# Softplus sums, projected rows and convolution weights in the Mamba stage of a hybrid network

## The chip, the cores and the metric

One core of a Trainium2 chip runs the whole network in one program. The metric is device time in microseconds from start to end of the program; a profiled execution also gives a trace of every instruction. The engines are TensorE (PE, matrix products into PSUM banks; PEld is its weight load), VectorE (DVE), ScalarE (ACT), GpSimd (POOL) and SyncE (SP, which here only issues DMAs). ACT and POOL also have DMA queues.

## The reference

The network has four layers on an image batch of 2 x 256 x 32 x 32. Layer 0 adds two Mamba blocks to a group norm; layer 1 is a 7 x 7 dilated kernel attention; layers 2 and 3 are attention and mixtures of experts. Only layer 0, and the preparation of layer 1's convolution weights that is done beside it, concern the change. Cut to what matters:

```
xr = u @ in_w + in_b                      # u: (b, 1024, 256)
xs, res = split(xr, 2)                    # 512 channels each
xs = silu(depthwise_conv4(xs) + conv_b)
dt, Bm, Cm = split(xs @ xproj_w, [16, 32])
delta = softplus(dt @ dt_w + dt_b)
dA  = exp(delta[..., None] * A)           # A: (512, 16)
dBu = delta[..., None] * Bm * xs[..., None]
h_t = dA_t * h_(t-1) + dBu_t              # scan over the 1024 tokens
y   = sum_n h_t * C_t + xs * Dp
out = (y * silu(res)) @ out_w + out_b
xt  = xt + layernorm(out)                 # twice: m1, then m2 (channels flipped)
```

Layer 1 convolves x with w1 (128 x 256 x 7 x 7), then with w2 (49 x 128); the kernel multiplies the two weights into one set of 49 taps first.

## The kernel before

**Tiling.** The 2048 tokens are four chunks j of 512 (TC). The 512 inner channels are four blocks dc of 128 partitions (NDC = 4). Two blocks of four chunks make eight *units*. Each unit runs `scan`: for each of 16 states n and each dc, ACT makes the decay `da` = exp(delta * A) into PSUM (L468), POOL makes the input `h` = du * b for two dc at once (L461), and VectorE scans h in place (L472). `rest(n)` then transposes h by PE into PSUM banks `ht` (L440, three banks), and VectorE (for two of the n ACT, L447) multiplies by C and adds to `ya` (L449). Six `h` tiles, three `da` banks and four `b` tiles are in turn; `b` comes by SP (L457) from DRAM, where the front has put it.

**Slots.** Each scan is one slot, 64 per unit. In the 63 slots between, `paced` pulls steps of generators: the *front* of the next unit (projection in, convolution, softplus), the *back* of the unit before (gate, skip, projection out, layer norm, residual), the weights of the next block, and `aside`, which is `Taps.make`. Each entry of `steps` is (generator, how many steps, first slot, end slot). The numbers in `layer0` set which work stands near which scan. They give the order in which the program is written; a planner of the framework then orders each engine's instructions by its own estimates of cost, with the written order as the priority, and gives out the buffers. On the chip each engine runs its list in that order.

**The front** (`front`, 22 head steps and 16 softplus steps) computes softplus from x = dt @ dt_w + b as max(x, 0) + ln(1 + e) with e = exp(-|x|). To keep the digits of small e, it adds e - ((e + 1) - 1). `e` lies in the buffer tag `pre`, `ln` in the tag `gate`, and `w` in `du` (one, one and two buffers). The four operations of each dc are at L405 (w = e - w), L407 (ln + w), L409 (delta + ln) and L411 (delta * xs); they run on POOL, except in the very first front (`alone`), where nothing else runs yet and VectorE does them. The rounding step is two ACT operations (L403, L404), or one on VectorE if alone.

**The back** (`back`) takes 9 steps for gate and y in slots 0 to 35 and 7 more in slots 40 to 61: four products into two PSUM banks of the pool `ps_mm` (tag `mm`, two banks for all matmul results), then `net.norm_rows` over the four row tiles straight from those banks (L160, L161 statistics, L150 square root, L151 and L166 factors, L168 result into `o`), then two steps of transposing (L179), scaling (L540) and adding to `xt` on POOL (L543, and L548 for the second block).

**Convolution weights** (`Taps.make`): 28 parts of four (or two) 128 x 128 pieces. Each part is loaded by SP (L686, two loads ahead), transposed by PE (L700), copied by ACT (L702) in one step; in the next step it is multiplied with w2 (L706), copied (L711) and written to DRAM by SP (L714). The last unit's `load` reads these rows back (L740) into the buffers of pre, xs, delta and du, for `convolve` (L762), which runs beside the last scan and, with `both`, beside the last back: there one step of the back is pulled after every three convolution steps.

Of the kernel before, what the change touches and what calls it, by code (L numbers as in the profile page):

```python
# [233 lines left out]
class Mamba:  # L234
# [58 lines left out]
    def front(self, j, alone=False):  # L293
# [104 lines left out]
        for dc in range(NDC):  # L398
            w = du[:, dc, :]
            if alone:  # L400
                nc.vector.tensor_scalar(w, e[:, dc, :], 1.0, -1.0, ALU.add, ALU.add)
            else:
                nc.scalar.activation(w, e[:, dc, :], AF.Identity, bias=net.one)  # L403
                nc.scalar.activation(w, w, AF.Identity, bias=net.minus_one)  # L404
            eng.tensor_sub(w, e[:, dc, :], w)  # L405
            yield
            eng.tensor_add(ln[:, dc, :], ln[:, dc, :], w)  # L407
            yield
            eng.tensor_add(delta[:, dc, :], delta[:, dc, :], ln[:, dc, :])  # L409
            yield  # L410
            eng.tensor_mul(w, delta[:, dc, :], xs[:, dc, :])  # L411
            yield
# [72 lines left out]
    def back(self, j):  # L485
# [33 lines left out]
        found = []  # L519
        for i in range(TPC):  # L520
# [11 lines left out]
            found.append(a)  # L532
            yield
        tiles = [o[:, i, :] for i in range(TPC)]
        net.norm_rows(tiles, found, nc.scalar)
        yield
        for cc in range(NCC):
# [37 lines left out]
def layer0(net, x, x_dram, m1, m2, load_image, taps, conv_dram, lg):  # L575
# [5 lines left out]
    with (  # L581
# [32 lines left out]
        for u, (m, j) in enumerate(units):  # L614
# [48 lines left out]
class Taps:  # L663
# [11 lines left out]
    def make(self, psum, dram):  # L675
# [17 lines left out]
        for i, (u, k) in enumerate(parts):  # L693
# [3 lines left out]
            n = min(4, 14 - k)  # L697
# [3 lines left out]
            wt = pool.tile([P, TC], F32, tag="w1t", name=f"w1ts_{u}_{k}", bufs=1)  # L701
# [8 lines left out]
            out = pool.tile([P, 4, NTAP], F32, tag="taps", name=f"taps_sb_{u}_{k}", bufs=3)  # L710
# [3 lines left out]
            nc.sync.dma_start(self.made[u][:, k : k + n, :], out[:, :n, :])  # L714
# [1028 lines left out]
```

## Time and profile before

| | |
|---|---|
| median of 3 runs | 2186.85 us (2185.29 to 2189.43) |
| the profiled execution | 2188.29 us, its span 2186.6 us |
| first scan, last scan | 53.3 us, 1030 us |
| starts of the eight units | 53.3, 165.3, 292.3, 418.75, 543.2, 664.4, 789.1, 913.8 us |
| last back and end of the first convolution | 1034 to 1110 us |
| VectorE in 52 to 1036 us | 925.2 us busy |
| ACT in 52 to 1036 us | 681.5 us busy |
| POOL in 52 to 1036 us | 768.9 us busy |
| softplus on POOL, L405, L407, L409, L411 | 28 each; 1184, 1273, 1271, 1273 ns |
| h on POOL, L461 | 254; 2364 ns |
| decay on ACT, L468 | 512; 690 ns |

How to read it: a group's line in the profile names the source line, the engine, the operation, the tile written and the tiles read, the shapes and the count; then busy time and the mean of one in ns; then how long the engine stood idle just before such instructions, and which instruction's end released it. The table by stretches lists busy time (and instructions) of PE, PEld, DVE, ACT and POOL, the granted clock of PE as a share of full speed, the DMA share and GB/s. In the timeline a line is a start, a duration, the engine, the line and the tiles.

### The profile page before, as it was taken

How to read it: one execution, taken by the hardware profiler on the slowest of the kernel's cores; microseconds unless marked ns; L12 is line 12 of the kernel's file. 1: busy time of each engine (PE TensorE's matmuls, PEld its weight loads, DVE VectorE, ACT ScalarE, POOL GpSimd, SP SyncE). 2: the span in 40 equal slices, each digit the busy share in tenths (PEclk: the TensorE clock that was granted, in tenths of full speed). 3: DMA queues.
4: the chain of work that ended last, by engine and by line, in shares of the span. 5: the costliest groups of instructions: out<-in, count | busy, mean ns of one | idle time of the engine just before them, and what ended most of it. 6: DMA issues, size and time to landing. Idle time of an engine off the chain costs nothing.

```text
span 2186.6 us, 27311 instructions
## 1 busy us (share of the span) xinstructions
PE 1894.0 (87%) x9652; PEld 1335.5 (61%) x9652; DVE 1400.3 (64%) x2210; ACT 959.2 (44%) x1610; POOL 1028.9 (47%) x726
## 2 busy tenths in 40 slices
PE   6888898898978888788999989949999599859996
PEld 2464555556555655454646556539999467649995
DVE  6999998999999999899005475752222544432223
ACT  4676677767777767645013454411111132301111
POOL 3796787959698686965025420012332000023331
PEclk9869889898989889899999999969999799979997
DMA  2121121111212111310030100028998200059997
GB/s 106 45 68 39 37 69 35 58 35 45 62 47 60 38 49 35 85 42 17 0 64 1 48 15 10 20 82 306 326 329 323 82 10 10 20 206 327 329 323 292
DMA packets 90499, 223.87 MB, mean 102 GB/s; under 512 B 35467, under 2 KB 51728, under 8 KB 79732
## 3 DMA queue, kind: packets, MB, share of 16 engines
q1 hardware_dynamic: 77636, 198.29, 27.1%
q0 software_dynamic: 7728, 19.15, 2.9%
q10 hardware_dynamic: 4992, 4.59, 0.7%
q8 instruction: 81, 1.33, 0.3%
q14 instruction: 62, 0.51, 0.1%
HBM read 204.60 MB, written 19.37 MB: 102 GB/s over the span
## 4 chain that ended last, share of the span: by engine, by line
PE 32%; DVE 22%; issue 19%; POOL 11%; ACT 10%; DMA 5%; POOLq 0%; SPq 0%; DVEq 0%; ACTq 0%
DVE m_h L472 11%; DVE m_ya L449 6%; PE acc L762 3%; POOL x L1520 3%; POOL l_yd L1570 3%; PE m_ht L440 3%; PE early_acc L762 3%; PE av L1276 3%; ACT m_da L468 2%; PE sc L1250 2%; DMA l_yd<-y,target 2%; POOL m_h L461 2%; PE h L1099 2%; PE m_xd_ps L351 1%; PE w L1108 1%
## 5 line engine op out<-in xcount | busy, mean ns | idle before, releaser
L461 POOL TENSOR_TENSOR m_h<-m_du,m_b 128x1024 f32<-128x1024 f32 x254 | 594.5, 2364 | 196.0 <-PE m_ht L440 95.8
L440 PE MATMUL m_ht<-ident,m_h 128*128 128x128 f32 x2048 | 361.2, 305 | 119.4 <-DVE m_ya L449 83.9
L440 PEld LDWEIGHTS m_ht<-ident,m_h 128*128 128x128 f32 x2048 | 259.5, 154 | 317.8 <-DVE m_ya L449 112.7
L468 ACT ACTIVATE m_da<-m_delta,m_aneg 128x512 f32<-128x512 f32 x512 | 349.5, 690 | 220.8 <-DVE m_h L472 220.1
L1520 POOL DMA_INDIRECT x<-l_zd,source x82 | 84.8, 1034 | 573.1 <-DVE source L1465 217.1
L449 DVE SCALAR_TENSOR_TENSOR m_ya<-m_ht,m_ct,m_ya 128x512 f32<-128x512 f32 x448 | 320.2, 733 | 18.4 <-PE m_ht L440 17.5
L472 DVE TENSOR_TENSOR_SCAN m_h<-m_da,m_state,m_h 128x512 f32<-128x512 f32 x256 | 318.7, 1271 | 14.7 <-POOL m_h L461 8.7
L472 DVE TENSOR_TENSOR_SCAN m_h<-m_da,m_h 128x512 f32<-128x512 f32 x256 | 303.3, 1210 | 23.6 <-ACT m_da L468 13.1
L1550 PEld LDWEIGHTS h<-xts,we 128*128 128x128 f32 x2528 | 298.4, 194 | 7.1 <-issue 3.4
L1550 PE MATMUL h<-xts,we 128*128 128x128 f32 x2528 | 299.4, 277 | 2.2 <-issue 1.7
L1557 DVE TENSOR_TENSOR hid<-hid,h 128x512 f32<-128x512 f32 x79 | 54.3, 688 | 258.9 <-PE h L1550 258.9
L1556 ACT ACTIVATE hid<-h 128x512 f32<-128x512 f32 x79 | 47.2, 598 | 384.6 <-issue 324.0
L1564 PE MATMUL o<-we,hid 128*128 128x256 f32 x632 | 150.4, 380 | 2.2 <-DVE y L1569 1.6
L1570 POOL DMA_INDIRECT l_yd<-y,target x79 | 79.3, 1003 | 142.6 <-DVE y L1569 136.3
L1564 PEld LDWEIGHTS o<-we,hid 128*128 128x128 f32 x632 | 113.7, 190 | 15.7 <-DVE y L1569 2.8
L336 PE MATMUL m_conv<-m_pre,m_taps 128*128 128x512 f32 x240 | 114.6, 596 | 6.7 <-ACT m_gate L498 5.6
L762 PE MATMUL early_acc<-x,early 128*98 128x448 f32 (+21 forms) x308 | 97.0, 447 | 0.0
L762 PE MATMUL acc<-x,pair 128*98 128x416 f32 (+21 forms) x308 | 93.6, 452 | 0.0
L1569 DVE COPY y<-o 128x256 f32<-128x256 f32 x79 | 33.6, 425 | 69.6 <-PE o L1564 69.6
L309 PE MATMUL m_in<-x,m_in_sb 128*128 128x512 f32 x128 | 68.8, 663 | 9.8 <-ACT m_pre L313 6.9
L762 PEld LDWEIGHTS acc<-x,pair 128*98 128x98 f32 x308 | 47.7, 167 | 39.9 <-issue 34.5
L528 PE MATMUL m_out<-m_out_sb,m_xs 128*128 128x256 f32 x256 | 68.7, 397 | 0.0
(318 smaller groups left out, 2843.3 us busy)
## 6 DMA issues: line engine op xcount, KB each, us to landing
we<-in_l_experts_dram SPq DMA_DIRECT2D x82, 1536.0 KB
m_b<-m_bd SPq DMA_DIRECT2D x128, 256.0 KB
w<-in_l_w_dram SPq DMA_DIRECT2D x21, 256.0 KB
l_zd<-l_z SPq DMA_DIRECT2D x7, 512.0 KB
l_yl<-l_yd SPq DMA_DIRECT2D x10, 256.0 KB
l_yl<-l_yd ACTq DMA_DIRECT2D x10, 256.0 KB
early<-taps SPq DMA_DIRECT2D x7, 343.0 KB
pair<-taps SPq DMA_DIRECT2D x7, 343.0 KB
```

The source lines that it names most:

```text
L309: nc.tensor.matmul(ps, lhsT=self.in_sb[:, kc, mc * P : (mc + 1) * P], rhs=self.xt[:, kc, tok], start=(kc == 0), stop=(kc == NCC - 1),)
L336: nc.tensor.matmul(ps, lhsT=self.taps[:, dc * 4 + k, :], rhs=pre[:, dc, k : k + TC], start=(k == 0), stop=(k == 3),)
L440: nc.tensor.transpose(ps[:, dc * P : (dc + 1) * P], hs[dc // G][:, dc % G, i * P : (i + 1) * P], net.ident,)
L449: nc.vector.scalar_tensor_tensor(ya[:, i, :], ps, c, ya[:, i, :], ALU.mult, ALU.add)
L461: (nc.vector if start and n == 0 else nc.gpsimd).tensor_mul(h, du[:, g * G : (g + 1) * G, :], b.unsqueeze(1).to_broadcast(half))
L468: nc.scalar.activation(da, delta[:, dc, :], AF.Exp, scale=self.aneg[:, i : i + 1])
L472: nc.vector.tensor_tensor_scan(h, da, h, 0.0 if first else state[:, n, dc : dc + 1], ALU.mult, ALU.add)
L762: nc.tensor.matmul(a[:, lo - 16 * k : hi - 16 * k, co : co + n], lhsT=lhsT, rhs=self.x[:, kc, b, lo - r0 : hi - r0, ci : ci + n], start=(u ...
L1520: nc.gpsimd.indirect_dma_start(out=x, out_offset=None, in_=zd[:, :], in_offset=bass.IndirectOffsetOnAxis(ap=source[:, g : g + 1], axis=0), ...
L1550: nc.tensor.matmul(ps[:, at], lhsT=w12[:, s, kc, at], rhs=xt[:, kc * P : (kc + 1) * P], start=(kc == 0), stop=(kc == NCC - 1),)
L1564: nc.tensor.matmul(ps[:, :C], lhsT=ht[:, mc * P : (mc + 1) * P], rhs=w[:, 8 + mc, :], start=(mc == 0), stop=(mc == NHC - 1),)
L1570: nc.gpsimd.indirect_dma_start(out=yd[g], out_offset=bass.IndirectOffsetOnAxis(ap=target[:, g : g + 1], axis=0), in_=y, in_offset=None, bo ...
```

## The change

- Softplus: e - ((e + 1) - 1) is now got as e plus (1 - (e + 1)) on ACT. The three additions per dc become one PSUM sum on PE: identity matmuls of delta, e, ln and w into a bank of `ps_mm`. ACT copies the bank to `delta`; POOL keeps the product with xs. The 12 steps stand in slots 38 to 54.
- In the first front, VectorE keeps the subtraction, PE sums delta, ln and w (banks of `ps_ht` for odd dc), and VectorE multiplies straight from PSUM.
- The back copies each pair of projected rows out of PSUM to `o` by ACT as soon as it is complete. Statistics are taken from `o`, one row tile per step; the factors and the in-place results are steps of their own. It has ten steps in slots 38 to 62 instead of seven in 40 to 61.
- `Taps.make` uses 35 parts of three (or two) pieces; the rows are written by the ACT queue; ten (twelve in the first unit) steps stand in slots 24 to 63 instead of nine (twelve) in 40 to 63.

```diff
             if alone:
                 nc.vector.tensor_scalar(w, e[:, dc, :], 1.0, -1.0, ALU.add, ALU.add)
+                nc.vector.tensor_sub(w, e[:, dc, :], w)
             else:
                 nc.scalar.activation(w, e[:, dc, :], AF.Identity, bias=net.one)
-                nc.scalar.activation(w, w, AF.Identity, bias=net.minus_one)
-            eng.tensor_sub(w, e[:, dc, :], w)
-            yield
-            eng.tensor_add(ln[:, dc, :], ln[:, dc, :], w)
-            yield
-            eng.tensor_add(delta[:, dc, :], delta[:, dc, :], ln[:, dc, :])
-            yield
-            eng.tensor_mul(w, delta[:, dc, :], xs[:, dc, :])
+                nc.scalar.activation(w, w, AF.Identity, scale=-1.0, bias=net.one)
+            yield
+
+            pool, tag = (self.ps_ht, "ht") if alone and dc % 2 else (self.ps_mm, "mm")
+            ps = pool.tile([P, TC], F32, tag=tag, name=f"{m}_sp_{j}_{dc}")
+            parts = (delta, ln, du) if alone else (delta, e, ln, du)
+            for k, a in enumerate(parts):
+                nc.tensor.matmul(
+                    ps, lhsT=net.ident, rhs=a[:, dc, :], start=(k == 0), stop=(k == len(parts) - 1)
+                )
+            nc.scalar.copy(delta[:, dc, :], ps)
+            yield
+            eng.tensor_mul(w, ps if alone else delta[:, dc, :], xs[:, dc, :])
             yield
...
         o = self.one.tile([P, TPC, C], F32, tag="o", name=f"{m}_o_{j}")
-        found = []
+        tiles = [o[:, i, :] for i in range(TPC)]
+        mv = net.small.tile([P, TPC, 2], F32, tag="ln_mv", name="ln_mv")
+
+        def stats(i):
+            st = net.small.tile([P, 6], F32, tag="ln_st", name="ln_st")
+            nc.vector.bn_stats(out=st, in_=tiles[i])
+            nc.vector.bn_aggr(out=mv[:, i, :], in_=st)
+
...
-            found.append(a)
-            yield
-        tiles = [o[:, i, :] for i in range(TPC)]
-        net.norm_rows(tiles, found, nc.scalar)
+
+            if i % 2:
+                nc.scalar.copy(
+                    o[:, i - 1 : i + 1, :], ps.rearrange("p (i c) -> p i c", c=C)
+                )
+            if i > 1:
+                stats(i - 2)
+            yield
+        stats(2)
         yield
+        stats(3)
+        rs = net.small.tile([P, TPC], F32, tag="ln_rs", name="ln_rs")
+        net.rstd(rs, mv[:, :, 1])
+        off = net.small.tile([P, TPC], F32, tag="ln_off", name="ln_off")
+        nc.vector.scalar_tensor_tensor(off, mv[:, :, 0], -1.0, rs, ALU.mult, ALU.mult)
+        yield
+        for i, a in enumerate(tiles):
+            nc.scalar.activation(
+                a, a, AF.Identity, scale=rs[:, i : i + 1], bias=off[:, i : i + 1]
+            )
+            if i % 2:
+                yield
...
-            steps += [(f, 16, 38, 62) for f in fronts] + [(b, 7, 40, 61) for b in done]
+            steps += [(f, 12, 38, 54) for f in fronts] + [(b, 10, 38, 62) for b in done]
             steps += [(rest, 1, 62, 63)]
             if u + 1 < len(units):
-                n = 9 if u else 12
-                steps += [(islice(aside, n), n, 40, 63)]
+                n = 10 if u else 12
+                steps += [(islice(aside, n), n, 24, 63)]
...
-        parts = [(u, k) for u in range(7) for k in range(0, 14, 4)]
+        parts = [(u, k) for u in range(7) for k in range(0, 14, 3)]
...
-            n = min(4, 14 - k)
-            w = pool.tile([P, 4, P], F32, tag="w1", name=f"w1_{u}_{k}", bufs=3)
+            n = min(3, 14 - k)
+            w = pool.tile([P, 3, P], F32, tag="w1", name=f"w1_{u}_{k}", bufs=3)
             nc.sync.dma_start(
-                w[:, :n, :], self.w1[:, u, k // NCC : (k + n) // NCC].rearrange("p v c o -> p (v c) o")
+                w[:, :n, :], self.w1[:, u].rearrange("p v c o -> p (v c) o")[:, k : k + n]
             )
...
-            nc.sync.dma_start(self.made[u][:, k : k + n, :], out[:, :n, :])
+            nc.scalar.dma_start(self.made[u][:, k : k + n, :], out[:, :n, :])
```

More of the change, by code (lines that the diff above doesn't have):

```diff
@@ L696, in make @@
             w = loaded[i]
-            n = min(4, 14 - k)
+            n = min(3, 14 - k)
             ps = psum.tile([P, TC], F32, tag="mm", name=f"w1t_{u}_{k}")
@@ L700, in make @@
                 nc.tensor.transpose(ps[:, a * P : (a + 1) * P], w[:, a, :], net.ident)
-            wt = pool.tile([P, TC], F32, tag="w1t", name=f"w1ts_{u}_{k}", bufs=1)
+            wt = pool.tile([P, 3 * P], F32, tag="w1t", name=f"w1ts_{u}_{k}", bufs=1)
             nc.scalar.copy(wt[:, : n * P], ps[:, : n * P])
@@ L709, in make @@
                 )
-            out = pool.tile([P, 4, NTAP], F32, tag="taps", name=f"taps_sb_{u}_{k}", bufs=3)
+            out = pool.tile([P, 3, NTAP], F32, tag="taps", name=f"taps_sb_{u}_{k}", bufs=3)
             nc.scalar.copy(
```

## The prediction

> **What bounds the kernel now.** I read the busy times first, then the stretch that the change touches, then who waits in it, and last the timeline of a few unit ends.
>
> ```profile
> PE 1894.0 (87%) x9652; PEld 1335.5 (61%) x9652; DVE 1400.3 (64%) x2210; ACT 959.2 (44%) x1610; POOL 1028.9 (47%) x726
> ...
> 52.00:1036.00 984.00, 838.63 (x3893) 531.55 (x3892) 925.15 (x1063) 681.46 (x1102) 768.93 (x417) 0.89 0.17 48
> ```
>
> The second line is the table by stretches (columns PE, PEld, DVE, ACT, POOL). Over the whole span PE looks like the bound; inside layer 0's scans (52 to 1036 us) VectorE is, with 925 of 984 us. The change touches only this layer.
>
> ```profile
> L449 DVE SCALAR_TENSOR_TENSOR m_ya<-m_ht,m_ct,m_ya 128x512 f32<-128x512 f32 x448 | 320.2, 733 | 18.4 <-PE m_ht L440 17.5
> L472 DVE TENSOR_TENSOR_SCAN m_h<-m_da,m_state,m_h 128x512 f32<-128x512 f32 x256 | 318.7, 1271 | 14.7 <-POOL m_h L461 8.7 <-ACT m_da L468 5.9
> L472 DVE TENSOR_TENSOR_SCAN m_h<-m_da,m_h 128x512 f32<-128x512 f32 x256 | 303.3, 1210 | 23.6 <-ACT m_da L468 13.1 <-POOL m_h L461 10.5
> ```
>
> VectorE's work is scans and sums, which the change leaves alone. What it can win is the idle before them: 18.4 + 14.7 + 23.6 and 1.9 before L516, 58.6 us together. The waits split it:
>
> ```profile
> DVE m_h L472 <- POOL m_h L461: 19.2, 13, 4.9
> DVE m_h L472 <- ACT m_da L468: 19.0, 23, 2.5
> DVE m_ya L449 <- PE m_ht L440: 17.5, 26, 2.2
> ```
>
> Then where. I cut each of the eight units (first scans at 53.3, 165.3, 292.3, 418.75, 543.2, 664.4, 789.1, 913.8; end 1034) into its 64 slots and took VectorE's busy time per stretch. For the fifth unit, slots 38-46, 46-54, 54-62 and 62-64:
>
> ```profile
> 615.20:630.30 15.10, 13.40 (x80) 10.36 (x79) 13.88 (x20) 15.04 (x22) 15.02 (x9) 1.00 0.14 40
> 630.30:645.50 15.20, 9.32 (x44) 5.94 (x42) 14.78 (x20) 11.13 (x22) 14.96 (x10) 0.78 0.24 77
> 645.50:660.60 15.10, 12.72 (x73) 11.07 (x72) 12.96 (x17) 10.12 (x22) 14.83 (x11) 0.66 0.10 32
> 660.60:664.40 3.80, 3.07 (x15) 2.02 (x16) 3.13 (x5) 3.03 (x9) 3.72 (x4) 1.00 0.32 109
> ```
>
> POOL has no pause, VectorE loses 2.14 + 0.67 = 2.81 us in the last ten slots, and PE pauses in the second stretch. The last ten slots of the first seven units lose 2.02, 2.14, 2.78, 2.22, 2.81, 2.09 and 4.50 us, and the first twelve slots of the last two units 2.67 and 1.88: 23.1 us lost at **hand-overs**. Slots 38-54, the **middle**, lose 0.8, 3.3, 1.7, 1.9, 1.6, 1.6 and 1.1: 12.0 us. One hand-over closely:
>
> ```profile
> 908.70 1.28 POOL L409 TENSOR_TENSOR m_delta<-m_delta,m_ln 128x512 f32<-128x512 f32 x1
> 910.06 1.27 POOL L411 TENSOR_TENSOR m_du<-m_delta,m_xs 128x512 f32<-128x512 f32 x1
> 911.28 4.66 POOL L461 TENSOR_TENSOR m_h<-m_du,m_b 128x1024 f32<-128x1024 f32 x2
> ...
> 910.01 0.69 ACT L498 ACTIVATE m_gate<-m_g,cols_sb 128x512 f32<-128x512 f32 x1 [6.57 <-POOL m_delta L409]
> ...
> 911.32 1.22 DVE L472 TENSOR_TENSOR_SCAN m_h<-m_da,m_h 128x512 f32<-128x512 f32 x1 [2.50 <-ACT m_da L468]
> ```
>
> ACT stood 6.57 us behind POOL's last softplus sum (the gate needs ln's buffer), the decay in its queue behind it came late, and VectorE stood 2.50 us. POOL's softplus chain is what ends last there.
>
> **The change, part by part.** Costs come from these rows:
>
> ```profile
> L405 POOL TENSOR_TENSOR m_du<-m_e,m_du 128x512 f32<-128x512 f32 x28 | 33.2, 1184 | 0.0
> L407 POOL TENSOR_TENSOR m_ln<-m_ln,m_du 128x512 f32<-128x512 f32 x28 | 35.6, 1273 | 1.1
> L409 POOL TENSOR_TENSOR m_delta<-m_delta,m_ln 128x512 f32<-128x512 f32 x28 | 35.6, 1271 | 1.5
> L702 ACT COPY w1ts<-w1t 128x512 f32<-128x512 f32 (+1 forms) x28 | 14.8, 529 | 5.5 <-PE w1t L700 5.1 <-ACT m_state L432 0.2
> ...
> 22.49 7.03 PE L336 MATMUL m_conv<-m_pre,m_taps 128*128 128x512 f32 x16
> ```
>
> (1) POOL loses 12 of its 16 softplus operations per front: 33.2 + 35.6 + 35.6 = 104.4 us, 14.9 us in each of seven units, and the last product is planned eight slots (15 us) earlier. In the last 24 slots (46 us) it then has 12 products of 2.36, 4 of 1.27 and 2 adds of 1.27: 36 us, so it gets ahead. Of the 23.1 us, the waits put down to POOL (19.2 less 6.1 behind the tap diagonals at 344 and 361 us, which stay) are 13.1, and some 8 are decays that came late. Bounds: 8 (a third) to 23.1. I take **-16**, most of what these two explain, because PE and ACT get fuller and some of it returns with another releaser. What is late next there: PE's backlog from (2).
>
> (2) PE gains, per unit, 4 sums of 4 matmuls 128x512. The 16 instructions above took 7.03 us, 0.44 each, and a float matmul is two of them (64 products on L309, 128 instructions): 32 x 0.43 = 13.8 us, 96 us in all. They queue before later transposes (L440), for which L449 waits. PE in slots 38-46 then has 32 transposes (3.9 us, 0.49 per four), 40 out-projection instructions of 0.217 (8.7), two sums (6.9) and some taps (1.0): 20.5 us in 15.2, 5.3 us behind, and catches up until about slot 56, where it now pauses. Cover: three m_ht banks and six m_h tiles, which let VectorE scan on while sums wait. Without cover it is 5.3 less the 1.6 us that PE stands in this stretch, 3.7 per unit, +26. With full cover 0. The nearest row is the stretch of slots 26-38, where PE is 98% busy (22.8 of 23.3 us) and VectorE loses about 2.1 us in twelve slots; the middle loses 1.7 today. ACT belongs here too: per unit 4 copies of the sums and 2 of the out rows at 0.57 and 5 DMA issues at 0.31 (the ACT queue's issue of m_bd), 5 us, in a stretch where it is already 15.04 of 15.10 busy; its decays are queued behind these. I take +1.2 us per unit for both, **+8.4**.
>
> [...] The clock shows 0.66 and 0.78 in the stretches above, and 0.50 from 520 to 535 us, where PE runs mostly L440. [...]
>
> (3) Convolution weights: 35 parts of three instead of 28 of four, from slot 24 on. Copies stay equal (a 384-wide copy for a 512-wide one). Some 3.6 of ten steps, 2 us of PE, move per unit to slots 24-38, where PE is 98% busy; they leave the end, where they crowd. Bounds 0 to 7 x 2 = 14; I take **+2**, since VectorE loses only 2.1 of 23.3 us there. The last nine steps now run in the seventh unit instead of none; their rows are read first in the eighth, behind loads of early tiles that wait for that unit's last product anyway (issued at 918 us). Moving the 35 writes from SP's queue to ACT's: 0 for SP, because POOL never waits for m_b in layer 0; the ACT issues are counted.
>
> [...]
>
> (4) Out rows copied from PSUM: the statistics cost 418 ns from PSUM and 416 from SBUF (L160 on m_out and on t), so no price on VectorE; two banks, held in the second unit from 241 and 254 to 279 us, come free after two steps each, so taps need not crowd into the end (278 to 292 us now). This gain is in (1).
>
> (5) First front: eight VectorE adds of 0.68 go (5.4 us); four sums of three matmuls come, 24 x 0.43 = 10.3 us on PE, which stands from 43 to 50 us. Two of the sums need the m_mm banks, which hold the next front's rows until ACT empties them at 49.3 us behind VectorE's last L405; that one now comes some 4 us earlier. The first scan moves from 53.3 to about 50. Bounds -5.4 to +3 (sums late at half clock); I take **-3**.
>
> (6) End of the layer: the last back half has 19 steps instead of 16, pulled once per three of 56 convolution steps, 18 pulls; the last transposes come behind the convolution (PE never idle 1052 to 1110 us). r, two adds of 1.27 on POOL end near 1114 instead of 1106.3; the next convolution starts at 1116.6 behind its weights' load. Only the xk transposes that fill 1111 to 1116 move back: **+1.5**, bounds 0 to 4.
>
> **The sum**: -16 + 8.4 + 2 - 3 + 1.5 = -7.1 us. The profiled execution took 2188.29 (span 2186.6 and 1.7 around it), 1.4 above the median; its span becomes 2179.5. From the median 2186.85 that is **2180**.
>
> **Rivals.**
> - *PE becomes the bound of the middle.* Place: slots 38-50 of seven units. For it: the 5.3 us of backlog, and ACT at 15.04 of 15.10. Against: slots 26-38 with PE as full lose only 2.1. Price +26 in place of +8.4: 10.5 us slower than before, 2197. It decides from 2.2 us per unit ((16 + 3 - 3.5) / 7).
> - *An even trade.* The planner that orders the instructions lets the sums slip past slot 54, and only 8 us of the hand-overs return: -8 + 8.4 + 2 - 3 + 1.5 = +0.9, 2188. For it: today's last product is planned for slot 61 and ran at slots 61 to 62 (287.0, 660.8 and 910.1 us); against: POOL's 14.9 us are gone wherever the sums land.
> - *Everything is covered*: -23.1 - 3 + 1.5 = -24.6, 2162. Against: PE at 98% has nowhere cost nothing.
>
> **Chances.** Forecast 0.42 (its own range 2168 to 2182), everything covered 0.10, even trade 0.20, PE bound 0.28. A measurement of this kernel tells about 0.2% (4.4 us) from no change: faster 0.52, same 0.20, slower 0.28. The range 2161 to 2198 leaves out about one in ten on the slow side and a little on the fast one.
>
> **What would show it.** Right: POOL with pauses in slots 54-64 and no VectorE wait for L461 there; first scan near 50 us; the clock near 1.00 in slots 46-54; VectorE's idle in layer 0 near 49 us. Wrong: L449 behind L440 well above 17.5 us, or L472 behind L468 above 19.0 in slots 42-50. The prediction fails if the middle loses over 2.2 us more per unit, or if hand-overs keep over half of their 23 us.

## The result, and the profile after

The changed kernel takes **2219.86 us** (median of 4 runs, 2214.84 to 2220.98), the kernel before 2186.07 (4 runs beside it): ratio **1.0151, interval 1.0136 to 1.0166**. It is slower by 1.5%, where the forecast was 2180. The profiled execution took 2214.84 us, the lowest of the four, with a span of 2212.9; it shows 26.3 us of loss against the span of 2186.6 before. The accounts by slots below are of these 26.3 us; the other 7.5 of the 33.8 between the medians stand in no profile. Lines have moved: L440 is now L446, L449 L455, L461 L467, L468 L474, L472 L478, L512 L518, L516 L522. New are L412 (the sums), L415 (their copy), L417 (GpSimd's product) and L530 and L559 (the rows' statistics and factors).

First the page's busy times, then the stretch that holds the scans of layer 0 in the table by stretches:

```profile
PE 1947.8 (88%) x9900; PEld 1349.7 (61%) x9900; DVE 1400.9 (63%) x2202; ACT 987.1 (45%) x1672; POOL 925.1 (42%) x642
```

```profile
50.00:1056.00 1006.00, 884.80 (x4116) 542.35 (x4115) 927.49 (x1061) 706.63 (x1160) 665.93 (x332) 0.96 0.17 47
```

GpSimd is relieved as planned (768.9 to 665.9 us), TensorE gained 46 us, the clock rose from 0.89 to 0.96. VectorE does the same work (925 and 927 us), but its stretch is 22 us longer (1006 against 984). So the loss is idle time of VectorE. The groups and the waits:

```profile
L455 DVE SCALAR_TENSOR_TENSOR m_ya<-m_ht,m_ct,m_ya 128x512 f32<-128x512 f32 x448 | 318.6, 731 | 31.5 <-PE m_ht L446 30.7
L478 DVE TENSOR_TENSOR_SCAN m_h<-m_da,m_state,m_h 128x512 f32<-128x512 f32 x256 | 317.0, 1266 | 16.5 <-POOL m_h L467 9.3
L478 DVE TENSOR_TENSOR_SCAN m_h<-m_da,m_h 128x512 f32<-128x512 f32 x256 | 301.8, 1207 | 27.6 <-POOL m_h L467 14.7
```

```profile
DVE m_ya L455 <- PE m_ht L446: 30.7, 37, 2.9
DVE m_h L478 <- POOL m_h L467: 24.0, 15, 3.6
DVE m_h L478 <- ACT m_da L474: 19.5, 22, 1.8
```

Behind TensorE's transposes VectorE now waits 30.7 us (17.5 before), behind GpSimd's products 24.0 (19.2). Where in a unit, is seen by cutting the eight units into their slots again, as 64 equal parts of each unit's time; VectorE's idle time, summed over the units, in us (each entry is the length of the stretches less VectorE's busy time in them):

| slots | 0-12 | 12-26 | 26-38 | 38-46 | 46-54 | 54-64 | sum |
|---|---|---|---|---|---|---|---|
| before | 5.1 | 9.7 | 12.9 | 7.3 | 4.7 | 19.0 | 58.6 |
| after | 2.0 | 7.3 | 25.9 | 25.1 | 16.0 | 2.3 | 78.5 |

The hand-over is as good as free of idle time now; slots 26 to 54 lose 42 us more. The fifth unit, stretches for slots 26-38, 38-46, 46-54, 54-62 and 62-64 (columns: length, PE, PEld, DVE, ACT, POOL, clock, DMA share, GB/s):

```profile
604.30:628.40 24.10, 20.19 (x104) 12.96 (x103) 19.50 (x24) 12.08 (x25) 14.90 (x10) 0.90 0.17 41
628.40:644.50 16.10, 16.10 (x60) 11.52 (x60) 10.12 (x12) 13.59 (x19) 7.38 (x4) 0.72 0.12 37
644.50:660.50 16.00, 16.00 (x73) 10.45 (x73) 13.81 (x21) 13.49 (x27) 10.59 (x5) 1.00 0.14 41
660.50:676.60 16.10, 14.25 (x89) 10.40 (x88) 15.67 (x21) 13.74 (x28) 14.75 (x9) 1.00 0.41 105
676.60:680.60 4.00, 3.14 (x13) 1.36 (x12) 4.00 (x5) 2.48 (x6) 4.00 (x3) 1.00 0.16 53
```

TensorE is busy for all of 16.10 and all of 16.00 us, while VectorE stands 6.0 and 2.2. In the same stretches before, TensorE worked 13.40 and 9.32. VectorE is busy throughout the last ten slots but for 0.4 us, where it lost 2.81.

Only the seventh unit is like this one: in both, slots 38-46 run at a clock of 0.72 and 0.73, and VectorE loses 8.2 and 8.1 us in slots 38 to 54. The other five units lose 3.8 to 6.7 there; their clock in slots 38-46 is 0.88 to 1.00, and TensorE is not busy all the time in them. The fourth unit, slots 38-46 and 46-54:

```profile
499.80:515.90 16.10, 14.51 (x76) 10.09 (x76) 13.79 (x17) 15.95 (x22) 10.68 (x6) 1.00 0.16 50
515.90:532.00 16.10, 15.46 (x74) 10.29 (x72) 14.20 (x21) 12.35 (x21) 10.32 (x6) 1.00 0.16 51
```

Here ScalarE is the fullest engine in the first stretch (15.95 of 16.10 us). By what VectorE waited for, slots 38 to 54 of the first seven units have 15.7 us behind GpSimd's products (none before), 12.3 behind TensorE's transposes (5.8 before) and 12.8 behind ScalarE's decays (6.8 before). The hand-over into the last unit, in the timeline:

```profile
931.41 0.67 ACT L504 ACTIVATE m_gate<-m_g,cols_sb 128x512 f32<-128x512 f32 x1
...
934.57 2.54 POOL L573 TENSOR_TENSOR x<-x,m_r 128x512 f32<-128x512 f32 x2
...
937.29 2.44 DVE L478 TENSOR_TENSOR_SCAN m_h<-m_da,m_state,m_h 128x512 f32<-128x512 f32 x2
```

The gate on ScalarE no longer stands 6.57 us behind softplus on GpSimd, and the unit's first scan has no idle time before it.

**Where TensorE gets behind.** TensorE's timeline in the same unit, before slot 38:

```profile
617.87 1.05 PE L518 MATMUL m_y<-ident,m_ya 128*128 128x128 f32 x8
618.76 1.06 PE L518 MATMUL m_y<-ident,m_yb 128*128 128x128 f32 x8
619.74 1.12 PE L380 MATMUL m_dt<-m_xd,m_dt_sb 16*128 16x512 f32 x2
620.79 0.77 PE L446 MATMUL m_ht<-ident,m_h 128*128 128x128 f32 x5
623.92 0.90 PE L730 MATMUL w1t<-ident,w 128*128 128x128 f32 x3 [2.37 <-DVE m_xs L522]
624.62 1.91 PE L446 MATMUL m_ht<-ident,m_h 128*128 128x128 f32 x8
...
633.32 3.78 PE L541 MATMUL m_out<-m_out_sb,m_xs 128*128 128x256 f32 x8
```

The weights' transposes (L730), now among the skip products, need one of the two `mm` banks. The bank is held by y until VectorE has multiplied it by the gate (L522), and that stands behind three scans in VectorE's own order. TensorE stands 2.37 us, with transposes of h ready behind L730 in its list. In the whole trace these waits are

```profile
PE w1t L730 <- DVE m_xs L522: 13.2, 8, 4.3
```

After this one the clock is down, seen in the table by stretches:

```profile
622.00:624.00 2.00, 0.07 (x1) 0.08 (x2) 2.00 (x4) 1.32 (x3) 0.03 (x1) 0.92 0.10 26
624.00:627.00 3.00, 3.00 (x12) 2.63 (x13) 1.92 (x3) 1.71 (x4) 1.82 (x1) 0.50 0.25 68
...
633.00:636.00 3.00, 3.00 (x7) 2.19 (x7) 2.28 (x3) 2.97 (x4) 3.00 (x2) 0.50 0.00 1
636.00:638.00 2.00, 2.00 (x12) 1.67 (x11) 0.25 (x1) 1.99 (x3) 0.62 (x1) 0.67 0.10 37
638.00:641.00 3.00, 3.00 (x11) 1.50 (x10) 3.00 (x4) 1.58 (x3) 0.00 (x0) 1.00 0.24 63
```

For 13 us TensorE is wholly busy at half speed; eight products of the out projection take 3.78 us, where they take 1.99 at a clock of 1.00 (sums_rows, 649.50). The sums then follow upon this backlog. The seventh unit repeats it. In the third, a wait of 4.3 us goes with a clock of 0.79 in slots 26 to 38; after the other waits, 0.64 to 1.31 us each, the clock stays at 1.00 for the next 4 us.

### The profile page after: what moved, and what is told of

Same layout as the page of the kernel before. It is cut to its first block, busy times and chain, and to the rows that moved or that the text cites. A ratio compares the mean times of both kernels' runs of the same rounds, so it can differ in the third digit from the quotient of the medians.

```text
span 2212.9 us, 27828 instructions
## 1 busy us (share of the span) xinstructions
PE 1947.8 (88%) x9900; PEld 1349.7 (61%) x9900; DVE 1400.9 (63%) x2202; ACT 987.1 (45%) x1672; POOL 925.1 (42%) x642
## 4 chain that ended last, share of the span: by engine, by line
PE 31%; DVE 18%; issue 18%; POOL 9%; DMA 4%; ACT 4%; POOLq 0%; ACTq 0%; DVEq 0%
DVE m_h L478 8%; DVE m_ya L455 5%; POOL x L1550 3%; PE acc L792 3%; POOL l_yd L1600 3%; PE m_ht L446 3%; PE av L1306 3%; PE sc L1280 2%; DMA l_yd<-y,target 2%; PE h L1129 2%; PE m_out L541 2%; PE early_acc L792 2%; PE m_sp L412 2%; PE w L1138 1%; DMA x<-l_zd,source 1%
## 5 line engine op out<-in xcount | busy, mean ns | idle before, releaser
L467 POOL TENSOR_TENSOR m_h<-m_du,m_b 128x1024 f32<-128x1024 f32 x254 | 596.0, 2369 | 295.2 <-PE m_ht L446 131.6
L474 ACT ACTIVATE m_da<-m_delta,m_aneg 128x512 f32<-128x512 f32 x512 | 349.9, 690 | 201.4 <-DVE m_h L478 200.1
L446 PEld LDWEIGHTS m_ht<-ident,m_h 128*128 128x128 f32 x2048 | 247.7, 147 | 272.6 <-DVE m_ya L455 98.0
L446 PE MATMUL m_ht<-ident,m_h 128*128 128x128 f32 x2048 | 326.9, 288 | 80.5 <-DVE m_ya L455 53.7
L455 DVE SCALAR_TENSOR_TENSOR m_ya<-m_ht,m_ct,m_ya 128x512 f32<-128x512 f32 x448 | 318.6, 731 | 31.5 <-PE m_ht L446 30.7
L478 DVE TENSOR_TENSOR_SCAN m_h<-m_da,m_state,m_h 128x512 f32<-128x512 f32 x256 | 317.0, 1266 | 16.5 <-POOL m_h L467 9.3
L478 DVE TENSOR_TENSOR_SCAN m_h<-m_da,m_h 128x512 f32<-128x512 f32 x256 | 301.8, 1207 | 27.6 <-POOL m_h L467 14.7
L1594 PEld LDWEIGHTS o<-we,hid 128*128 128x128 f32 x632 | 113.7, 190 | 15.7 <-DVE y L1599 2.8
```

Of the source, the lines that this page charges most:

```text
L446: nc.tensor.transpose(ps[:, dc * P : (dc + 1) * P], hs[dc // G][:, dc % G, i * P : (i + 1) * P], net.ident,)
L455: nc.vector.scalar_tensor_tensor(ya[:, i, :], ps, c, ya[:, i, :], ALU.mult, ALU.add)
L467: (nc.vector if start and n == 0 else nc.gpsimd).tensor_mul(h, du[:, g * G : (g + 1) * G, :], b.unsqueeze(1).to_broadcast(half))
L474: nc.scalar.activation(da, delta[:, dc, :], AF.Exp, scale=self.aneg[:, i : i + 1])
L478: nc.vector.tensor_tensor_scan(h, da, h, 0.0 if first else state[:, n, dc : dc + 1], ALU.mult, ALU.add)
L1594: nc.tensor.matmul(ps[:, :C], lhsT=ht[:, mc * P : (mc + 1) * P], rhs=w[:, 8 + mc, :], start=(mc == 0), stop=(mc == NHC - 1),)
```

## The experiments

The table gives each time, its difference to the kernel before on the same chip, and the ratio with its interval.

| run | us | less before | ratio |
|---|---|---|---|
| the change | 2219.86 | +33.8 | 1.0151 [1.0136, 1.0166] |
| taps_late | 2200.79 | +18.1 | 1.0077 [1.0053, 1.0100] |
| pool_sums | 2232.02 | +49.3 | 1.0216 [1.0179, 1.0253] |
| half_sums | 2208.62 | +25.9 | 1.0113 [1.0078, 1.0148] |
| only_taps | 2207.67 | +24.9 | 1.0109 [1.0078, 1.0141] |
| only_sums | 2212.21 | +26.3 | 1.0122 [1.0105, 1.0140] |
| only_rows | 2192.63 | +6.8 | 1.0034 [1.0022, 1.0046] |
| sums_rows | 2209.66 | +23.8 | 1.0120 [1.0087, 1.0152] |
| sums_rows_slow | 2168.93 | -16.9 | 0.9919 [0.9900, 0.9937] |
| change_sums62 | 2192.29 | +6.1 | 1.0048 [1.0020, 1.0077] |
| change_sums62_taps40 | 2173.23 | -13.0 | 0.9942 [0.9920, 0.9964] |
| sums62 | 2221.30 | +35.1 | 1.0164 [1.0143, 1.0184] |
| sums_rows_46 | 2180.51 | -5.7 | 0.9985 [0.9969, 1.0001] |
| tight_two | 2182.12 | -2.8 | 0.9978 [0.9968, 0.9989] |
| tight_no_w | 2216.05 | +31.1 | 1.0135 [1.0111, 1.0159] |
| tight_late_product | 2199.51 | +14.6 | 1.0052 [1.0028, 1.0076] |
| best_late_product | 2185.64 | +0.7 | 1.0004 [0.9992, 1.0016] |
| loose_two | 2168.99 | -16.2 | 0.9928 [0.9905, 0.9950] |

Each time is the median of 4 to 10 runs.

**The change with its taps later** (taps_late):

```diff
-                steps += [(islice(aside, n), n, 24, 63)]
+                steps += [(islice(aside, n), n, 40, 63)]
```

> The changed kernel with one number put back: the convolution-weight steps stand in slots 40 to 63 instead of 24 to 63. Theory S (the sums' 13.8 us of PE per unit make the loss; it is VectorE's idle in slots 38-54, 12.0 us before and 41.1 after): the tail gets fuller, so VectorE's idle in slots 38-54 stays at 35 to 50 us and the time stays at 2210 to 2225. Theory T (the taps' transposes stand in PE's list among the y products and wait for a PSUM bank that VectorE's m_xs products free, 13.2 us of PE waits, with all later transposes behind them; PE then falls to half clock, 0.72 in slots 38-46 of the fifth unit): these waits go, VectorE's idle in slots 26-38 goes from 25.9 back to about 13 and the time falls by 13 us or more, to 2206 or less.

Against the kernel before, the loss falls from 33.8 to 18.1 us, by about half. VectorE's idle in slots 26 to 38 falls from 25.9 to 12.0, the value of before. The early taps are one fault. Slots 38 to 54 keep 38.6 of their 41.1 us, so that the sums, or something else, are another.

**The sums back on GpSimd** (pool_sums), with 16 steps in slots 38 to 62 and the rest of the change kept:

```diff
+            if not alone:
+                nc.gpsimd.tensor_add(ln[:, dc, :], ln[:, dc, :], w)
+                yield
+                nc.gpsimd.tensor_add(ln[:, dc, :], ln[:, dc, :], e[:, dc, :])
+                yield
+                nc.gpsimd.tensor_add(delta[:, dc, :], delta[:, dc, :], ln[:, dc, :])
+                nc.gpsimd.tensor_mul(w, delta[:, dc, :], xs[:, dc, :])
+                yield
+                continue
```

> The changed kernel with softplus' three additions back on POOL (sixteen steps in slots 38 to 62); the first front, the out rows and the taps stay as changed. Theory S: VectorE's idle in slots 38-54 falls from 41 to 12-18 us and the hand-overs get back 10 to 20 us of theirs: 2186 to 2200. Theory T: slots 26-38 keep their 25.9 us and part of the middle stays: 2200 to 2215.

Slower than the change by 15 us: neither theory had that. With the taps early, GpSimd's adds are worse than TensorE's sums, and in the same slots 38 to 62 by more (change_sums62 below, 43 us less). So taking the sums off TensorE is no cure; why it costs so much is open, and whether their place in slots 38 to 54 is a fault this run doesn't tell.

**Two matmuls for each sum, in the change** (half_sums); e and its rounding term are left out of the sum:

```diff
-            parts = (delta, ln, du) if alone else (delta, e, ln, du)
+            parts = (delta, ln, du) if alone else (delta, ln)
```

> The changed kernel with two matmuls per sum instead of four (delta and ln; e and its rounding counterpart are left out of the sum, ACT still computes the latter), so 6.9 us of PE per unit instead of 13.8, everything else equal. Theory S: the loss is PE's time, so about half of the middle's 29 us comes back: 2200 to 2207. Theory T: the waits before slot 40 stay, 2212 to 2220.

8 us come back, a time between the two theories. With the taps still early, slots 26 to 38 keep 22.9 us of idle time and slots 38 to 46 26.1.

**One part of the change at a time, on the kernel before**: the taps alone (only_taps), the sums alone with their slots 38 to 54 (only_sums), the rows alone (only_rows). Their edits are the hunks of the change that bear on each part, so that of the lists of steps only these differ:

```diff
# only_taps
-                n = 9 if u else 12
-                steps += [(islice(aside, n), n, 40, 63)]
+                n = 10 if u else 12
+                steps += [(islice(aside, n), n, 24, 63)]
# only_sums
-            steps += [(f, 16, 38, 62) for f in fronts] + [(b, 7, 40, 61) for b in done]
+            steps += [(f, 12, 38, 54) for f in fronts] + [(b, 7, 40, 61) for b in done]
# only_rows
-            steps += [(f, 16, 38, 62) for f in fronts] + [(b, 7, 40, 61) for b in done]
+            steps += [(f, 16, 38, 62) for f in fronts] + [(b, 10, 38, 62) for b in done]
```

> The kernel before with the taps' part of the change alone (parts of three, written by the ACT queue, from slot 24 on). Theory S: PE has room in slots 40-63 without the sums, so within 3 us of the kernel before. Theory T: the bank waits come with the taps alone: PE waits of taps transposes on m_xs above 8 us, VectorE's idle in slots 26-38 about 20 us instead of 12.9, and 2194 to 2205.

> The kernel before with the sums alone (four-matmul sums on PE in twelve steps of slots 38 to 54, first front included); out rows and taps as before. Putting the taps back to slot 40 won 19 us of the loss and left 18 over the kernel before. Theory S (the sums' chain PE sum, ACT copy, POOL product holds POOL's list up: 38.9 us of POOL waits on the copy with the h products behind them): 2195 to 2205. Theory R (the out rows' part makes the rest: its copies and in-place results on ACT, its ten steps from slot 38 on): 2170 to 2185, since the hand-overs' 20 us come back.

> The kernel before with the out rows' part alone (copies out of PSUM, ten steps in slots 38 to 62). Theory S: within 4 us of the kernel before, or a little faster since the taps get banks earlier. Theory R: 2195 to 2205, VectorE's idle in slots 38-54 above 20 us instead of 12.

Each part alone makes the kernel slower. In only_sums, slower than either theory had it, the idle time stands in slots 0 to 12 (26.2 us, 5.1 before), as in sums62 below. In the waits of only_taps stands the line that the timeline above showed once, as theory T had it:

```profile
PE w1t L700 <- DVE m_xs L516: 15.0, 7, 5.4
```

**Sums and rows without the taps part**, the sums in slots 38 to 54 (sums_rows) and, with the one number altered, in 38 to 62 (sums_rows_slow; the name speaks of the steps' pace):

```diff
-            steps += [(f, 12, 38, 54) for f in fronts] + [(b, 10, 38, 62) for b in done]
+            steps += [(f, 12, 38, 62) for f in fronts] + [(b, 10, 38, 62) for b in done]
```

> The changed kernel with the whole taps part as before (parts of four, SP's queue, slots 40 to 63): sums and out rows. Beside taps_late (2200.8) it tells what parts of three and the ACT queue's writes cost: theory that they cost nothing, 2198 to 2204; theory that ACT's issues and the extra steps cost, 2185 to 2195.

> As sums_rows with the twelve steps of the sums in slots 38 to 62 instead of 38 to 54. Theory S by density (too much PE and ACT in slots 38-46): VectorE's idle in slots 38-54 falls by 10 us or more, hand-overs stay below 8 us, 8 us or more faster than sums_rows. Theory that the density does not matter: within 4 us of sums_rows.

sums_rows came out above both of its ranges. The one number is worth 41 us, and the second kernel is faster than the kernel before. VectorE's idle by slots:

| slots | 0-12 | 12-26 | 26-38 | 38-46 | 46-54 | 54-64 | sum |
|---|---|---|---|---|---|---|---|
| sums_rows | 2.0 | 12.1 | 13.0 | 12.8 | 29.7 | 8.1 | 77.8 |
| sums_rows_slow | 1.1 | 5.7 | 13.8 | 11.4 | 5.6 | 0.7 | 38.3 |

In slots 46 to 54, 24.3 of the 29.7 are waits for GpSimd's h. TensorE, GpSimd and VectorE there, in the fifth unit of sums_rows:

```profile
643.86 0.93 PE L446 MATMUL m_ht<-ident,m_h 128*128 128x128 f32 x7
644.70 1.12 PE L412 MATMUL m_sp<-m_delta,ident 128*128 128x512 f32 x2
645.66 1.02 PE L412 MATMUL m_sp<-m_e,ident 128*128 128x512 f32 x2
646.52 1.02 PE L412 MATMUL m_sp<-m_ln,ident 128*128 128x512 f32 x2
647.38 1.02 PE L412 MATMUL m_sp<-m_du,ident 128*128 128x512 f32 x2
648.24 0.71 PE L446 MATMUL m_ht<-ident,m_h 128*128 128x128 f32 x5
648.88 0.69 PE L537 MATMUL m_out<-rows_m_out_b,ones_row 1*128 1x256 f32 x2
649.50 1.99 PE L541 MATMUL m_out<-m_out_sb,m_xs 128*128 128x256 f32 x8
651.33 0.99 PE L736 MATMUL taps_ps<-w_sb,w1ts 128*128 128x49 f32 x8
652.15 1.05 PE L446 MATMUL m_ht<-ident,m_h 128*128 128x128 f32 x8
...
648.86 2.35 POOL L467 TENSOR_TENSOR m_h<-m_du,m_b 128x1024 f32<-128x1024 f32 x1 [3.66 <-ACT m_da L474]
...
651.25 2.34 DVE L478 TENSOR_TENSOR_SCAN m_h<-m_da,m_h 128x512 f32<-128x512 f32 x2 [2.99 <-POOL m_h L467]
```

From 643.9 to 653.2 us TensorE does not pause; in these 9 us there are only 20 transposes of h, little more than one state's 16, while a state has 7.9 us. One sum takes 3.5 us of TensorE, one row tile of the out projection 2.6. An `h` tile comes free when its transposes are done (GpSimd's products wait 114.4 us for them in layer 0 of sums_rows); GpSimd's next product stood 3.66 us, and VectorE 2.99 behind it. A wait of VectorE's for GpSimd's h of 2.1 to 3.8 us stands in slots 46 to 54 of each of the second to seventh units (in the fourth at 526.79, in the sixth at 782.10), and each time TensorE is busy without a pause through it and for the 6 us before it. (The profile puts GpSimd's wait down to a decay that ended at the same moment, 648.86, while TensorE's five transposes were running; which of the two ended last there it doesn't tell.)

**The same number in the change itself** (change_sums62), and **both numbers** (change_sums62_taps40: the edit above and that of taps_late):

> The change with one number altered: Softplus' 12 steps in slots 38 to 62 instead of 38 to 54; the taps still begin at slot 24. Theory D (density: twelve steps in 16 slots, each a chain from ScalarE over TensorE and ScalarE to a product on GpSimd, queue too close upon one another in the orders of TensorE and GpSimd): what separated the two kernels without the taps part, 2209.7 and 2168.9, is had here too, so 2219.9 - 41 = 2179, range 2172 to 2192, and VectorE's idle in slots 38 to 54 of the units falls from 41 us to under 25. Theory T (the taps from slot 24 are the larger fault, since they put TensorE behind before the sums begin): the time falls by less than 20, to 2200 to 2215, and slots 26 to 38 keep their 26 us.

> The change with two numbers altered: Softplus' 12 steps in slots 38 to 62, and the taps (parts of three, results stored by ScalarE's queue) in slots 40 to 63. Theory D with the taps' early start as a second, separate fault of some 19 us: 2219.9 - 41 - 19 = 2160, range 2155 to 2172; no worse than the 2168.9 with the taps part whole as before. Rival: the early taps had relieved slots 40 to 63, so that with all three jobs there TensorE has too much in them (its busy share reaches 98% and over in slots 38 to 54) and the time is 2175 to 2195.

| less before, us | taps from 24 | taps from 40 |
|---|---|---|
| sums 38 to 54 | +33.8 | +18.1 |
| sums 38 to 62 | +6.1 | -13.0 |

The two faults about add up: 28 and 31 us for the sums' slots, 16 and 19 for the taps' start. The sums' slots are worth less here than the 41 us that theory D took over, so that both times lie at the upper ends of its ranges (2192.3, and 2173.2 just outside). With both mended the change is faster than before by 13 us.

**The sums alone with slots 38 to 62** (sums62):

```diff
-            steps += [(f, 12, 38, 54) for f in fronts] + [(b, 7, 40, 61) for b in done]
+            steps += [(f, 12, 38, 62) for f in fronts] + [(b, 7, 40, 61) for b in done]
```

> The kernel before with the sums alone, 12 steps in slots 38 to 62; the out rows and the taps as before. Measured with slots 38 to 54: 2212.2. Theory D: 2212.2 - 41 = 2171, range 2164 to 2183. Rival R (the gain needs the rows' part, which frees PSUM banks of TensorE's outputs at once): without it the time is 2188 to 2205, no faster than before.

Theory D falls here, and R stands: without the rows part the kernel is 35 us slower than before, with it 17 us faster. TensorE around a hand-over of sums62:

```profile
527.71 1.99 PE L534 MATMUL m_out<-m_out_sb,m_xs 128*128 128x256 f32 x8
529.54 1.72 PE L446 MATMUL m_ht<-ident,m_h 128*128 128x128 f32 x12
533.10 1.31 PE L446 MATMUL m_ht<-ident,m_h 128*128 128x128 f32 x8 [1.84 <-DVE m_ya L455]
...
539.00 1.11 PE L446 MATMUL m_ht<-ident,m_h 128*128 128x128 f32 x4 [0.79 <-DVE m_ya L455]
539.91 1.06 PE L706 MATMUL w1t<-ident,w 128*128 128x128 f32 x4
...
544.26 1.91 PE L412 MATMUL m_sp<-m_delta,ident 128*128 128x512 f32 x2
545.97 1.91 PE L412 MATMUL m_sp<-m_e,ident 128*128 128x512 f32 x2
```

```profile
537.15 1.93 ACT L168 ACTIVATE m_o<-m_out,ln_off,ln_rs 128x256 f32<-128x256 f32 x4
```

The out rows stay in both `mm` banks until ScalarE's results at 537.15 to 539.08. From 529.5 to 539.9 TensorE has nothing but transposes of h, and pauses; the sums and the taps that need a bank come after, at half clock (0.50 from 536 to 548 us), and stand in the next unit's first slots (37.9 us of idle time in slots 0 to 12, against 1.1 in sums_rows_slow).

**As close, but later** (sums_rows_46):

```diff
-            steps += [(f, 12, 38, 54) for f in fronts] + [(b, 10, 38, 62) for b in done]
+            steps += [(f, 12, 46, 62) for f in fronts] + [(b, 10, 38, 62) for b in done]
```

> Sums and rows as changed, taps as before, the sums' 12 steps in slots 46 to 62: as close upon one another as in the change (16 slots), but ending where they ended before. Measured: 2209.7 with slots 38 to 54, 2168.9 with 38 to 62. Theory D (density decides): 2200 to 2215. Rival P (the place decides: the steps collide with what lies in slots 38 to 46, or their early end leaves the hand-over to others): 2165 to 2178. In between, 2180 to 2198: both have a part.

At the edge between both having a part and Rival P alone: 16 slots cost 30 us less eight slots later, where the out projection is done (in the fifth unit at 628.0, the first sum at 629.6), and 11 us more than 24 slots. The larger part is not the pace by itself but what else TensorE has in those slots.

**Which engine**: from sums_rows, two matmuls for each sum (tight_two, the edit of half_sums), no rounding passes on ScalarE (tight_no_w; the rounding term is not in the result and e is added twice instead), and GpSimd's product one sum later (tight_late_product).

```diff
# tight_no_w
-                nc.scalar.activation(w, e[:, dc, :], AF.Identity, bias=net.one)
-                nc.scalar.activation(w, w, AF.Identity, scale=-1.0, bias=net.one)
+                pass
...
-            parts = (delta, ln, du) if alone else (delta, e, ln, du)
+            parts = (delta, ln, du) if alone else (delta, e, ln, e)
# tight_late_product
-            eng.tensor_mul(w, ps if alone else delta[:, dc, :], xs[:, dc, :])
-            yield
+            if alone:
+                eng.tensor_mul(w, ps, xs[:, dc, :])
+                yield
+                continue
+            for k in ([dc - 1] if dc else []) + ([dc] if dc == NDC - 1 else []):
+                eng.tensor_mul(du[:, k, :], delta[:, k, :], xs[:, k, :])
+                yield
```

> Sums in slots 38 to 54 and rows as changed, taps as before (measured with four matmuls per sum: 2209.7; spread over 38 to 62: 2168.9), with two matmuls per sum, of the Relu and the logarithm: it leaves out e and its rounding term in the sum, ScalarE still makes the rounding term. Theory V (TensorE's volume in slots 38 to 54 is what is too much): half of the sums' 16 us a unit is gone, so most of the 41 us come back: 2172 to 2188. Theory A (ScalarE's chain of two passes and a copy for each sum) and theory O (the product waits at the head of GpSimd's order): at most a third comes back, 2195 to 2210.

> The same base (2209.7), four matmuls per sum as there, but ScalarE's two passes for the rounding term are left out, and e stands in its place in the sum: the rounding term is not in the result. ScalarE is relieved of 8 x 0.71 = 5.7 us a unit, and TensorE's last matmul of a sum waits for nothing of ScalarE's. Theory A: most of the 41 us come back, 2170 to 2188. Theories V and O: 2198 to 2210.

> The same base (2209.7) and the whole computation; only the order of steps is altered: GpSimd's product of one channel block is issued after the sum of the next block instead of after its own, so that it does not wait at the head of GpSimd's order for the copy that has only just been issued. Theory O: the waits of GpSimd's product on the copy fall from 39 us to under 15, VectorE's waits on GpSimd's products in slots 46 to 54 from 24 us to under 8, and the time is 2180 to 2192. Theories V and A: GpSimd then waits elsewhere, 2202 to 2214.

> Sums in slots 38 to 62 and rows as changed, taps as before (2168.9), with the products of GpSimd one sum later as in the run before. Theory O: a few us better, 2158 to 2167. Theories V and A: 2166 to 2173, no change beyond what is measured from run to run; worse than 2175 if the last two products, now both at the end, come too late for the next unit's first products of h.

TensorE's work for the sums explains two thirds (27 of 41 us); with it the waits of GpSimd's product on the copy fall too, from 39.4 to 11.3 us. Those waits are not the loss by themselves: in sums_rows_46 they are 41.3 us. ScalarE's passes explain nothing on balance (7 us slower without them): VectorE's idle in slots 38 to 46 falls from 12.8 to 7.1 us, and in slots 46 to 54 it rises from 29.7 to 37.7. The later product gains 9 us, between the theories, and not as expected: its waits on the copy stay at 38.9 us. In slots 46 to 54 VectorE's waits on GpSimd's h fall from 24.3 to 9.3. In the kernel with room (best_late_product) the same order costs 17 us, 19.1 of waits on h in slots 46 to 54: the price that was feared for the last two products.

**The fourth corner** (loose_two: two matmuls, slots 38 to 62):

> Two matmuls per sum as in the run with slots 38 to 54 (2182.1; it leaves out e and its rounding term in the sum), with the sums in slots 38 to 62, rows as changed, taps as before; with four matmuls there 2168.9. Theory V: with 24 slots TensorE had room for the four, so little is left to gain: 2158 to 2169, against 28 us in the tight slots. Rival (each matmul taken from TensorE is worth the same wherever it lies): another 20 to 28 us, 2140 to 2149.

| less before, us | 4 matmuls | 2 matmuls |
|---|---|---|
| sums 38 to 54 | +23.8 | -2.8 |
| sums 38 to 62 | -16.9 | -16.2 |

Half of the sums' products is worth 27 us in 16 slots and nothing in 24. TensorE's work for the sums costs time where it is bunched, and is free where it is spread. It is the bunch that counts, and not the share over all 16 slots: in slots 38 to 54 of the first seven units TensorE is busy 199.3 of 220.7 us (90%) in sums_rows, and 194.7 of 210.0 (93%) in sums_rows_slow. And with two matmuls the slots' number is still worth 13 us (-2.8 and -16.2); no run explains this third of the 41.

## Why the prediction failed

In the forecast's own terms, against the profiled executions (26.3 us longer span; idle time from the first table):

| step | forecast | measured |
|---|---|---|
| (1) hand-overs, slots 0-12 and 54-64 | -16 (8 to 23.1) | -19.8 (24.1 to 4.3) |
| (2) middle, slots 38-54 | +8.4 (0 to 26) | +29.1 (12.0 to 41.1) |
| (3) taps, slots 26-38 | +2 (0 to 14) | +13.0 (12.9 to 25.9) |
| slots 12-26 | none | -2.4 |
| (5) first scan | -3 (-5.4 to +3) | -3.4 (53.3 to 49.9) |
| (6) end of the layer | +1.5 (0 to 4) | +4.1 |
| VectorE's own work in the scans | none | +5.5 |

The sum of the right column is 26.1.

**Right**: what bounded the hand-overs, that they come back, the first scan, and the clock in slots 46 to 54 (1.00 in every unit; 0.78 to 0.85 before in the second to the seventh), a sign worked out from no row of before. Of the two rows that the forecast named as signs against it, L455 behind L446 rose from 17.5 to 30.7 us; L478 behind L474 stayed at 19.5 as a whole, but in slots 42 to 50, which the forecast had named, it rose from 6.4 to 9.4.

**The failed step is (2).** It priced TensorE's backlog at 1.2 us a unit, because six `h` tiles and three `ht` banks were to cover it and because slots 26 to 38, with TensorE 98% busy, lose only 2.1 us. Measured are 4.2 a unit (29.1 over seven), past the 2.2 at which the forecast said that it fails. Its bound was too low as well: 20.5 us of work in 15.2 leaves 5.3, and TensorE's pause of 1.6 is already used up in that, so that without cover it is 5.3 a unit (37 us), not 3.7. So the cover was small. Not all of the 29.1 is step (2) alone: 13.5 fall into the fifth and the seventh unit, where the half clock behind step (3) reaches into slots 38 to 46. But sums_rows, with the taps as before, has 42.5 us in the middle, and sums_rows_slow 17.0. ScalarE, which the forecast put into the same term, has 6.0 of the 29.1 (VectorE's waits for decays, 6.8 to 12.8).

The hand-over of sums_rows shows why the cover fails: in a bunch of 9 us the sums, the out rows and the taps stand among the transposes, the tiles come free late, and GpSimd and then VectorE wait. That the wait grows with every state over the 16 slots isn't shown. Slots 26 to 38 were full of work that just fits; their row tells what full costs, not what more than full costs. That it is TensorE's work for the sums that costs in 16 slots and not in 24, tight_two and loose_two show. As an estimate from the fifth unit before: its busy time times its clock in slots 38-46, 46-54 and 54-62 is 13.4, 7.3 and 8.4 us; with the sums' 13.8 that makes 34.5 us for the 30.3 of slots 38 to 54, and 42.9 for the 45.4 of slots 38 to 62. In the fifth unit of sums_rows the last of the four sums did slip past slot 54 (664.68 us, where the slot ends at 661.8).

This was the rival "PE becomes the bound of the middle", right in place and near in price (+26), with 0.28 of the chance. In kind it was right in part: more of the waits came by way of GpSimd's products than directly behind the transposes. Its time (2197) was too low, mostly because step (3) stood in it unaltered (11 us) and VectorE's own work was missing (5.5).

**Step (3) failed the same way.** It priced 2 us of added work by the same row, TensorE 98% busy and VectorE losing only 2.1. What came was a wait for a bank at the head of TensorE's order, 13.2 us of it in the trace of after, and in two units the clock that falls behind it (0.72 and 0.73 in slots 38 to 46). taps_late and the two numbers' table give 16 to 19 us.

**Step (4) priced the rows wrongly in kind.** The forecast had them as a convenience for the taps. By themselves they cost 7 us; with the sums in the same slots they are what frees the sums' banks, 52 us between sums62 and sums_rows_slow.

**Steps (6) and the rest** were mis-sized. TensorE stands longer at the layer's end than forecast (6.18 us before the next layer's first transposes, 1.22 before):

```profile
1138.88 0.71 PE L887 MATMUL xk<-ident,xs 128*128 128x128 f32 x2 [6.18 <-POOL xs L886]
```

Of VectorE's 5.5 us more work, up to 4.3 are the norm's factors (7.8 us for eight, one of them behind the scans, where they took 3.5), 978 ns where it was 441:

```profile
L559 DVE SCALAR_TENSOR_TENSOR ln_off<-ln_mv,ln_rs 128x4 f32<-128x4 f32 x8 | 7.8, 978 | 0.0
```

Why they take longer is open (161 to 2149 ns in after; in sums_rows_slow they mean 425). Open too is what the writes on ScalarE's queue, parts of three instead of four, and the planner's own order contribute: change_sums62_taps40 and sums_rows_slow, which differ by the parts and the queue, lie 4 us apart with intervals that overlap; taps_late and sums_rows, the same pair with the sums in slots 38 to 54, lie 6 apart the other way, overlapping too; and neither the parts nor the queue was tried alone.

**The best version** is sums_rows_slow, 0.9919 [0.9900, 0.9937]: the sums on TensorE, the rows out of PSUM, the taps as before, and the sums over slots 38 to 62. Its waits:

```profile
DVE m_ya L455 <- PE m_ht L446: 19.3, 26, 2.1
...
DVE m_h L478 <- ACT m_da L474: 9.2, 18, 1.2
DVE m_h L478 <- POOL m_h L467: 7.8, 7, 5.2
```

The hand-over's gain is kept (L478 behind POOL 7.8 us, before 19.2), and the wait behind TensorE's transposes is back near its 17.5.

## What to carry to other kernels

Moving work to an engine that is "off the bound" is to be priced slot by slot: add up that engine's work in the slots where it will stand, and where the sum is more than they hold, charge most of the excess (here 4.2 of 5.3 us a unit), not what the buffers might cover. Spread over half as many slots again, the same work turned a loss into a gain (+23.8 to -16.9 us).

A step moved earlier is to be asked which buffer it takes from whom. In an order that is fixed, an instruction that waits for a bank holds up everything behind it, and the pause can be followed by a loss of clock larger than itself, as in two of seven units here (a wait of 2.37 us each, then some 13 us at a clock of 0.50).

## What the runs showed of the hardware

After the pause of 2.37 us (621.6 to 623.9 in after) the clock was 0.50 for 13 us, though TensorE was busy all the time; that is some 6.7 us of work (half of 13.4) lost behind a 2.4 us wait. The clock fell at about 623.7, worked out from its mean of 0.92 over 622 to 624. Up to 632.2 us TensorE ran mostly transposes of h and of the weights (5.6 of 8.3 us), and full clock came back at about 637.3, some 5 us after the out projection's products began (632.17). In sums62 it ran only transposes and short products from 529.5 to 544.3, with a clock of 0.50 from 536 on, and full clock came back at about 548.5, some 4 us after the sums began (544.26). Whether the pauses, or what TensorE ran, set the clock in these two places, no run tested. Busy at half clock is what before shows too: from 483 to 487 us TensorE is busy all the time at 0.50.
